# Eight-expert feed-forward stage: second product with tokens on partitions, routing weight as a factor of the row

## The chip, the cores and the metric

The kernel runs on one core of a Trainium2 chip, in float32. The metric is the device time of one launch in microseconds (us). Engines are named as the profile names them: PE (matrix product) and PEld (its weight loads), DVE (vector), ACT (activations), POOL, and SP, which here only issues DMAs.

## The reference

The whole model is a chain of eight residual stages over x of shape (2, 512, 128): attention-like stages and feed-forward stages in turn. The change touches the second one, a feed-forward layer with eight experts of which each token uses two:

```python
xf = x.reshape(-1, D)                       # x is the layernorm of the running sum
scores = xf @ router_w.T
top_v, top_i = jax.lax.top_k(scores, TOP_K) # two of eight
routing_w = jax.nn.softmax(top_v, axis=-1)
out = jnp.zeros_like(xf)
for e in range(NUM_EXPERTS):
    w_e = jnp.sum(jnp.where(top_i == e, routing_w, 0.0), axis=-1)
    h = jax.nn.gelu(xf @ expert_w1[e].T, approximate=False)   # 128 -> 512
    out = out + h @ expert_w2[e].T * w_e[:, None]             # 512 -> 128
# x = x + out
```

Every expert is computed for every token, and the weight w_e is zero where the token did not choose it.

## The kernel before

The running sum X stays in SBUF as 128 partitions x 8 tiles of tokens x 128 features: four token tiles for each of the two batch elements b. The stages run one after the other: stage0 (cross attention with three iterations), stage1 (the eight experts, the one that changes), stage2 (attention with 16 heads), stage3 (experts with one shared matrix and small corrections), stage4 and stage6 (six-layer transformers), stage5 and stage7 (feed-forward stages).

Two things set the order of instructions. Inside `with nc.stretch()` a planner in the kernel records the operations, estimates durations and writes an order of its own; its instructions all carry line 356. Stage 0's iterations, stage 2 and the transformers run so. Outside a stretch, as in all of stage1, the instructions go straight to the framework's scheduler and carry line 124; the scheduler may interleave what does not depend on each other.

Stage1 first takes the layernorm of X, transposes it into nT (features on partitions, 512 tokens per b), computes the scores with the router matrix rw, finds the two best experts on DVE and builds W, the weight of each token for each expert, with tokens on partitions. Then it loops over the experts e and over b; one such pair is called a round below, and there are 16. A round does this:

- four first products of 128x128 weights and 512 tokens go in pairs into two-bank PSUM tiles (`banks()`, name big, two buffers), and one Gelu on ACT for each pair writes hT, hidden features on partitions, tokens along the row;
- a selector product spreads the weight of expert e over all partitions: sel holds one-hot columns of eight rows, wT holds W transposed, and the result is copied from PSUM to wb;
- four second products accumulate over the hidden chunks f into one bank yps (`bank()`, name ms, three buffers), with output features on partitions;
- DVE multiplies yps by wb into y, and POOL adds y to acc.

After the loop acc is transposed back by PE in eight pieces and added to X. An expert's weights, 512 KB, are one DMA on SP's queue into the tile ew, with three buffers; the matrix rw comes by ACT's queue. The tiles of stage1 lie in three pools (one for single tiles, one for double-buffered ones, the expert pool last), which take the SBUF space that the pools of stage0 gave back; a tile waits for what used its place before. Stage2's pools follow in the same way, and its weights wq, wkv and wo are loaded when the places are free.

In the profile one fp32 matmul is shown as two matmul records, each with a weight load of its own.

Of the kernel before, what the change touches and what calls it, by code (L numbers as in the profile page):

```python
# [11 lines left out]
F32 = mybir.dt.float32  # L12
# [3 lines left out]
ALU = mybir.AluOpType  # L16
# [3 lines left out]
P = 128  # L20
D = 128
B = 2
S = 512
NT = S // P
# [9 lines left out]
FC = DFF // P  # L34
# [325 lines left out]
class Kernel:  # L360
# [245 lines left out]
    def stage1(self):  # L606
        nc, X = self.nc, self.X
        E = 8
        with self.tc.tile_pool(name="s1", bufs=1) as one, self.tc.tile_pool(name="s1w", bufs=2) as two, \
                self.tc.tile_pool(name="s1e", bufs=3) as expert:  # L610
            rw = one.tile([P, E], F32, name="rw")
            nc.scalar.dma_start(rw, self.io["router"])
            sel = one.tile([E, E, P], F32, name="sel")
            nc.vector.tensor_copy(sel, self.ident[:E, :E].unsqueeze(2).to_broadcast([E, E, P]))
            nT = [one.tile([P, S], F32, name=f"nT1{b}") for b in range(B)]
            ps = self.bank()
            for b in range(B):
                nc.vector.tensor_copy(nT[b], self.transposed(self.normed(b, X)))
            for t in range(T):
                b, i = divmod(t, NT)  # L620
                nc.tensor.matmul(ps[:, t * E:(t + 1) * E], lhsT=nT[b][:, i * P:(i + 1) * P], rhs=rw, start=True, stop=True)
            sc = one.tile([P, T, E], F32, name="sc1")
            nc.vector.tensor_copy(sc.rearrange("p t e -> p (t e)"), ps[:, :T * E])
            v8, idx = self.top_experts(one, sc, 2)

            dv = one.tile([P, T], F32, name="dv")
            nc.vector.tensor_tensor(dv, v8[:, :, 1], v8[:, :, 0], ALU.subtract)
            nc.scalar.activation(dv, dv, AF.Exp)
            wt = one.tile([P, 2, T], F32, name="wt")
            nc.vector.tensor_scalar(wt[:, 0, :], dv, 1.0, None, ALU.add)  # L630
            nc.vector.reciprocal(wt[:, 0, :], wt[:, 0, :])
            nc.vector.tensor_tensor(wt[:, 1, :], dv, wt[:, 0, :], ALU.mult)
            W = one.tile([P, T, E], F32, name="W1")
            oh = one.tile([P, 2, T, E], F32, name="oh1")
            for k in range(2):
                self.one_hot(oh[:, k], idx[:, :, k])
                nc.vector.tensor_tensor(oh[:, k], oh[:, k], wt[:, k, :].unsqueeze(2).to_broadcast([P, T, E]), ALU.mult)
            nc.vector.tensor_tensor(W, oh[:, 0], oh[:, 1], ALU.add)
            wT = one.tile([E, B, S], F32, name="wT1")
            for b in range(B):  # L640
                ps = self.bank(E)
                for i in range(NT):
                    nc.tensor.transpose(ps[:, i * P:(i + 1) * P], W[:, b * NT + i, :], self.ident)
                nc.vector.tensor_copy(wT[:, b, :], ps)
            acc = one.tile([P, B, S], F32, name="acc1")
            for e in range(E):
                w = expert.tile([P, 1024], F32, name="ew")
                nc.sync.dma_start(w, self.io["w1"][e])
                for b in range(B):
                    hT = two.tile([P, FC, S], F32, name="hT1")  # L650
                    for pair in range(FC // 2):
                        ps = self.banks()
                        for j in range(2):
                            f = 2 * pair + j
                            nc.tensor.matmul(ps[:, j * S:(j + 1) * S], lhsT=w[:, f * P:(f + 1) * P], rhs=nT[b], start=True, stop=True)
                        nc.scalar.activation(hT[:, 2 * pair:2 * pair + 2, :].rearrange("p f s -> p (f s)"), ps, AF.Gelu)
                    wps = self.bank()
                    nc.tensor.matmul(wps, lhsT=sel[:, e, :], rhs=wT[:, b, :], start=True, stop=True)
                    wb = two.tile([P, S], F32, name="wb1")
                    nc.vector.tensor_copy(wb, wps)  # L660
                    yps = self.bank()
                    for f in range(FC):
                        nc.tensor.matmul(yps, lhsT=w[:, 512 + f * P:512 + (f + 1) * P], rhs=hT[:, f, :], start=f == 0, stop=f == FC - 1)
                    if e == 0:
                        nc.vector.tensor_tensor(acc[:, b, :], yps, wb, ALU.mult)
                    else:
                        y = two.tile([P, S], F32, name="y1")
                        nc.vector.tensor_tensor(y, yps, wb, ALU.mult)
                        nc.gpsimd.tensor_tensor(acc[:, b, :], acc[:, b, :], y, ALU.add)
            for b in range(B):  # L670
                pt = self.bank()
                for i in range(NT):
                    nc.tensor.transpose(pt[:, i * P:(i + 1) * P], acc[:, b, i * P:(i + 1) * P], self.ident)
                xb = X[:, b * NT:(b + 1) * NT, :]
                nc.vector.tensor_tensor(xb, xb, pt.rearrange("p (n d) -> p n d", d=D), ALU.add)


    def stage2(self):
# [788 lines left out]
```

## Time and profile before

| | |
|---|---|
| median of 3 runs | 3820.19 us (3816.91 to 3825.85) |
| the profiled execution: its own time, its span | 3818.73 us, 3817.0 us |
| granted PE clock, mean | 0.899 |
| PE busy | 3396.6 us, 89% of the span |
| DVE, ACT, POOL busy | 2449.4, 1762.7, 563.2 us |
| stage1, 163 to 314 us: PE, DVE, ACT, POOL busy | 141.25, 38.37, 35.55, 19.71 of 151 us |

The span is the time from the first to the last instruction; the time of a launch has a little more around it. Busy times are those of one profiled execution. In the lines of a group the columns are the source line, the engine, the operation, output <- inputs, the shapes and the count; after the bar come the busy time in us and the mean duration in ns; after the second bar the idle time of the engine just before these instructions and what ended it. In a timeline the columns are start and duration in us, engine, line, operation and tiles, count, and in brackets the idle time before.

### The profile page before, as it was taken

What the parts mean: (1) busy time and instruction counts of PE and PEld (TensorE: products, weight loads), DVE (VectorE), ACT (ScalarE), POOL (GpSimd) and SP (SyncE); (2) the same over time, 40 slices, a digit from 0 to 9 for tenths busy, and PEclk for the clock granted to TensorE, in tenths of its full rate; (3) what the DMA queues carried; (4) which work ended last, traced back from release to release, by engine and by line L of the source; (5) the groups of instructions that cost most, each with busy time, mean ns of one, the idle gap of its engine ahead of it and who ended that gap; (6) DMA issues with size and microseconds to landing.
All of it is one profiled execution on the core that took longest, in us unless ns stands there. A gap on an engine that the chain in (4) does not pass through costs nothing.

```text
span 3817.0 us, 56843 instructions
## 1 busy us (share of the span) xinstructions
PE 3396.6 (89%) x21539; PEld 1864.8 (49%) x21539; DVE 2449.4 (64%) x5712; ACT 1762.7 (46%) x3268; POOL 563.2 (15%) x516
## 2 busy tenths in 40 slices
PE   5598999889999999999999739999999999999937
PEld 3333555455555455554545425545455455554526
DVE  5514555377676776767677478677676767767532
ACT  1123545236454554545555314456454555545550
POOL 2214767210100000000000010000100001010000
PEclk8698999879898998999989768989899999989858
DMA  1000000100010000000000100010010001000002
GB/s 38 1 28 22 1 1 1 39 12 5 10 25 10 23 7 23 10 10 23 13 7 8 39 5 8 7 28 5 10 25 10 23 7 28 5 10 9 6 20 78
DMA packets 179494, 61.00 MB, mean 16 GB/s; under 512 B 169475, under 2 KB 173367, under 8 KB 177559
## 3 DMA queue, kind: packets, MB, share of 16 engines
q1 hardware_dynamic: 177400, 54.72, 6.4%
q8 instruction: 171, 2.80, 0.3%
q10 hardware_dynamic: 1519, 1.74, 0.1%
q0 software_dynamic: 304, 0.92, 0.1%
q14 instruction: 100, 0.82, 0.1%
HBM read 36.37 MB, written 0.52 MB: 10 GB/s over the span
## 4 chain that ended last, share of the span: by engine, by line
PE 72%; DVE 16%; POOL 4%; ACT 3%; issue 2%; DMA 1%; SPq 1%; DVEq 0%; ACTq 0%; POOLq 0%
PE ms L356 61%; PE ms L124 5%; DVE mx L356 4%; PE big L124 2%; PE av L356 2%; PE big L356 2%; POOL turned L356 2%; POOL p L356 1%; ACT p L356 1%; DVE ln_st L356 1%; DVE nrm L356 1%; POOL ln_rs L356 1%; DVE avT L356 1%; DVE Y L356 1%; SPq L356 1%
## 5 line engine op out<-in xcount | busy, mean ns | idle before, releaser
L356 ACT ACTIVATE p<-ms 128x512 f32<-128x512 f32 (+1 forms) x2304 | 1209.6, 614 | 768.5 <-PE ms L356 764.9
L356 DVE TENSOR_REDUCE mx<-ms 128x1 f32<-128x512 f32 (+2 forms) x2316 | 1281.7, 609 | 238.5 <-PE ms L356 234.4
L356 PE MATMUL ms<-kT,qT 29*128 29x512 f32 x3072 | 949.9, 678 | 30.3 <-DMA qT<-mxT 12.3
L356 PE MATMUL ms<-qT,kT 32*128 32x512 f32 (+1 forms) x3096 | 919.7, 632 | 3.2 <-DVE mx L356 2.7
L356 PEld LDWEIGHTS ms<-kT,qT 29*128 29x128 f32 x3072 | 403.9, 196 | 296.5 <-DVE mx L356 149.9
L356 PEld LDWEIGHTS ms<-qT,kT 32*128 32x128 f32 (+1 forms) x3096 | 376.8, 184 | 190.9 <-issue 61.0
L356 DVE STREAM_TRANSPOSE avT<-ms 128x512 f32<-128x512 f32 x192 | 137.5, 716 | 379.8 <-PE ms L356 379.8
L356 PE MATMUL ms<-kcT,qT 29*128 29x154 f32 x3072 | 353.4, 329 | 25.8 <-DVE mx L356 18.6
L356 POOL TENSOR_TENSOR ln_rs<-ln_ve,mhalf 128x4 f32<-128x4 f32 x96 | 97.5, 1019 | 1851.9 <-DVE ln_ve L356 1851.8
L356 PE MATMUL ms<-p,vp 128*32 128x512 f32 x3072 | 353.2, 600 | 0.7
L356 PE MATMUL ms<-qT,kcT 32*77 32x512 f32 x1536 | 343.6, 641 | 1.5 <-DVE mx L356 1.5
L356 PEld LDWEIGHTS ms<-kcT,qT 29*128 29x128 f32 x3072 | 301.6, 196 | 86.2 <-DVE mx L356 36.0
L356 POOL TENSOR_SCALAR p<-p,s 128x666 f32<-128x666 f32 x128 | 248.8, 1956 | 118.3 <-DVE s L356 118.3
L356 PE MATMUL ms<-p,vcp 77*32 77x512 f32 x1536 | 199.2, 650 | 0.6 <-DVE mx L356 0.5
L356 PEld LDWEIGHTS ms<-p,vp 128*32 128x32 f32 x3072 | 90.9, 110 | 220.7 <-issue 181.7
L356 ACT ACTIVATE nrm_t<-ms,gb 128x512 f32<-128x512 f32 x72 | 56.1, 779 | 290.6 <-PE ms L356 272.9
L356 PE MATMUL ms<-ident,nrm 128*128 128x128 f32 x344 | 83.5, 376 | 96.3 <-DVE nrm L356 79.2
L356 PEld LDWEIGHTS ms<-qT,kcT 32*77 32x77 f32 x1536 | 120.0, 148 | 94.5 <-ACT p L356 32.6
L356 DVE TENSOR_REDUCE m<-big 128x1 f32<-128x666 f32 x128 | 104.2, 847 | 83.0 <-PE big L356 83.0
L356 ACT ACTIVATE p<-big,m 128x666 f32<-128x666 f32 x128 | 103.7, 814 | 116.1 <-DVE m L356 115.3
L356 POOL TENSOR_TENSOR turned<-rope_a,rope_s 128x256 f32<-128x256 f32 x144 | 101.7, 730 | 358.6 <-DVE rope_s L356 358.5
L356 PE MATMUL ms<-nrm_t,lw 128*128 128x512 f32 x192 | 136.0, 874 | 1.7 <-ACT nrm_t L356 1.7
(336 smaller groups left out, 3534.9 us busy)
## 6 DMA issues: line engine op xcount, KB each, us to landing
lw<-in_layers SPq DMA_DIRECT2D x12, 1413.0 KB
ew<-in_w SPq DMA_DIRECT2D x24, 512.0 KB
qT<-rows SPq DMA_DIRECT2D x192, 64.0 KB
qT<-mxT SPq DMA_DIRECT2D x768, 2.0 KB
kT<-rows SPq DMA_DIRECT2D x96, 64.0 KB
wkv<-in_wkv SPq DMA_DIRECT2D x1, 1024.0 KB
f2b<-in_f2b SPq DMA_DIRECT2D x12, 64.0 KB
rv<-in_rows POOLq DMA_DIRECT2D x1, 640.0 KB, 6.5
```

Of the source, the lines that this page charges most:

```text
L124: return getattr(getattr(self._plan.real, self._name), method)(*a, **k)
L356: getattr(getattr(self.real, op.lane), op.method)(*op.a, **op.k)
```

## The change

The second product swaps its operands: a 128-token slice of hT is the stationary operand, and the 128 columns of the second weight matrix are streamed, so that the output has tokens on partitions, the layout of X. Each round then has 16 matmuls of 128 columns instead of four of 512. The routing weight is now one number per partition, so a single DVE instruction for each token tile multiplies the product by a column of W and adds it to X. The tiles sel, wT, wb, y and acc go, with the selector products, the transposes of W and of acc, and POOL's additions.

```diff
--- before.py
+++ after.py
@@ -610,8 +610,6 @@
                 self.tc.tile_pool(name="s1e", bufs=3) as expert:
             rw = one.tile([P, E], F32, name="rw")
             nc.scalar.dma_start(rw, self.io["router"])
-            sel = one.tile([E, E, P], F32, name="sel")
-            nc.vector.tensor_copy(sel, self.ident[:E, :E].unsqueeze(2).to_broadcast([E, E, P]))
             nT = [one.tile([P, S], F32, name=f"nT1{b}") for b in range(B)]
             ps = self.bank()
             for b in range(B):
@@ -636,13 +634,6 @@
                 self.one_hot(oh[:, k], idx[:, :, k])
                 nc.vector.tensor_tensor(oh[:, k], oh[:, k], wt[:, k, :].unsqueeze(2).to_broadcast([P, T, E]), ALU.mult)
             nc.vector.tensor_tensor(W, oh[:, 0], oh[:, 1], ALU.add)
-            wT = one.tile([E, B, S], F32, name="wT1")
-            for b in range(B):
-                ps = self.bank(E)
-                for i in range(NT):
-                    nc.tensor.transpose(ps[:, i * P:(i + 1) * P], W[:, b * NT + i, :], self.ident)
-                nc.vector.tensor_copy(wT[:, b, :], ps)
-            acc = one.tile([P, B, S], F32, name="acc1")
             for e in range(E):
                 w = expert.tile([P, 1024], F32, name="ew")
                 nc.sync.dma_start(w, self.io["w1"][e])
@@ -654,25 +645,15 @@
                             f = 2 * pair + j
                             nc.tensor.matmul(ps[:, j * S:(j + 1) * S], lhsT=w[:, f * P:(f + 1) * P], rhs=nT[b], start=True, stop=True)
                         nc.scalar.activation(hT[:, 2 * pair:2 * pair + 2, :].rearrange("p f s -> p (f s)"), ps, AF.Gelu)
-                    wps = self.bank()
-                    nc.tensor.matmul(wps, lhsT=sel[:, e, :], rhs=wT[:, b, :], start=True, stop=True)
-                    wb = two.tile([P, S], F32, name="wb1")
-                    nc.vector.tensor_copy(wb, wps)
+
                     yps = self.bank()
-                    for f in range(FC):
-                        nc.tensor.matmul(yps, lhsT=w[:, 512 + f * P:512 + (f + 1) * P], rhs=hT[:, f, :], start=f == 0, stop=f == FC - 1)
-                    if e == 0:
-                        nc.vector.tensor_tensor(acc[:, b, :], yps, wb, ALU.mult)
-                    else:
-                        y = two.tile([P, S], F32, name="y1")
-                        nc.vector.tensor_tensor(y, yps, wb, ALU.mult)
-                        nc.gpsimd.tensor_tensor(acc[:, b, :], acc[:, b, :], y, ALU.add)
-            for b in range(B):
-                pt = self.bank()
-                for i in range(NT):
-                    nc.tensor.transpose(pt[:, i * P:(i + 1) * P], acc[:, b, i * P:(i + 1) * P], self.ident)
-                xb = X[:, b * NT:(b + 1) * NT, :]
-                nc.vector.tensor_tensor(xb, xb, pt.rearrange("p (n d) -> p n d", d=D), ALU.add)
+                    for i in range(NT):
+                        for f in range(FC):
+                            nc.tensor.matmul(yps[:, i * D:(i + 1) * D], lhsT=hT[:, f, i * P:(i + 1) * P], rhs=w[:, 512 + f * D:512 + (f + 1) * D],
+                                             start=f == 0, stop=f == FC - 1)
+                    for i in range(NT):
+                        x = X[:, b * NT + i, :]
+                        nc.vector.scalar_tensor_tensor(x, yps[:, i * D:(i + 1) * D], W[:, b * NT + i, e:e + 1], x, ALU.mult, ALU.add)
 
 
     def stage2(self):
```

## The prediction

> **What bounds the kernel now.** I read the page's busy table first (PE 3396.6 us, 89% of the span), then its chain of waits: PE carries 72% of it, and line 124 (everything outside a planned stretch) only "PE ms 5%" and "PE big 2%". The change sits in one such stage, so I left the averages and took the groups and the timeline of 163 to 314 us. The groups:
>
> ```profile
> L124 PE MATMUL big<-nT,ew 128*128 128x512 f32 x128 | 62.2, 627 | 0.8 <-issue 0.8
> L124 PE MATMUL ms<-hT,ew 128*128 128x512 f32 x128 | 59.2, 605 | 0.0
> L124 ACT ACTIVATE hT<-big 128x1024 f32<-128x1024 f32 x32 | 32.8, 1024 | 115.7 <-PE big L124 115.7
> L124 PE MATMUL ms<-wT,sel 8*128 8x512 f32 x32 | 17.9, 640 | 0.0
> L124 POOL TENSOR_TENSOR acc<-acc,y 128x512 f32<-128x512 f32 x14 | 17.7, 1264 | 122.2 <-DVE y L124 89.1 <-issue 33.2
> ```
>
> PE has no idle to speak of; ACT, DVE and POOL all wait for it. Counts are twice the code's (64 second products per stage stand as 128): each fp32 matmul runs as two passes, each with its own weight load. So the stage ends when PE ends. One round (one expert, one batch element), in the timeline (start, duration, engine):
>
> ```profile
> 200.45 1.12 PE L124 MATMUL ms<-wT,sel 8*128 8x512 f32 x2
> 200.56 1.02 ACT L124 ACTIVATE hT<-big 128x1024 f32<-128x1024 f32 x1 [0.63 <-PE big L124]
> 201.50 3.70 PE L124 MATMUL ms<-hT,ew 128*128 128x512 f32 x8
> 202.04 0.19 PEld L124 LDWEIGHTS ms<-hT,ew 128*128 128x128 f32 x1 [0.24 <-issue]
> 202.47 0.19 PEld L124 LDWEIGHTS ms<-hT,ew 128*128 128x128 f32 x1 [0.24 <-issue]
> 205.04 3.60 PE L124 MATMUL big<-nT,ew 128*128 128x512 f32 x8
> 208.57 1.12 PE L124 MATMUL ms<-wT,sel 8*128 8x512 f32 x2
> ```
>
> From selector to selector 8.12 us. A 512-column pass starts every 0.43 us (202.04, 202.47). Sixteen passes are 6.85 us, so the selector's two passes, with the gaps at entering and leaving an 8-row product, take 1.26 us. They also give ACT time: the second Gelu (200.56 to 201.58) runs beside them.
>
> The stage's two ends:
>
> ```profile
> 162.86 0.34 ACTq L124 DMA_DIRECT2D rw<-in_router  x1
> 166.15 0.67 DVE L124 COPY sel<-ident 8x1024 f32<-8x1024 f32 x1
> 171.78 2.04 PE L124 MATMUL big<-nT,ew 128*128 128x512 f32 x2 [0.83 <-issue]
> ...
> 311.56 1.26 POOL L124 TENSOR_TENSOR acc<-acc,y 128x512 f32<-128x512 f32 x1 [6.85 <-DVE y L124]
> 312.88 0.66 PE L124 MATMUL ms<-ident,acc 128*128 128x128 f32 x4 [1.75 <-POOL acc L124]
> 313.70 0.33 SPq L124 DMA_DIRECT2D wkv<-in_wkv  x1
> 320.16 3.57 PE L356 MATMUL ms<-wkv,kv 128*111 128x512 f32 x4 [6.62 <-DMA wkv<-in_wkv]
> ```
>
> The last product ends near 310.54; y, POOL's addition and four transposes follow, and only then is stage 2's weight load wkv issued, for which PE waits. What moves the issue of wkv moves the rest of the kernel.
>
> **What the Trainium skill says.** "TensorE: Matmul & The Clock Gate", section "LDWEIGHTS (loading the stationary operand)": the cost goes by the columns loaded, about columns/1.2 ns, thus an estimated 107 ns for 128. Its "Step-by-step: what each phase is for": the next weights load while the present matmul streams. Both decide here, since the new product has a load for every 128 columns streamed. The trace agrees: two other places of this kernel run that shape (the same loop form at 980 us):
>
> ```profile
> 980.71 3.84 PE L356 MATMUL ms<-lw,hT 128*128 128x128 f32 x32
> 984.48 1.71 PE L356 MATMUL ms<-kcT,qT 29*128 29x154 f32 x32
> 3805.40 7.41 PE L124 MATMUL ms<-eo,put 128*128 128x128 f32 x64 [0.78 <-DVE eo L124]
> ```
>
> 32 passes take 984.48 - 980.71 = 3.77 us (0.118 each); 64 take 7.41 less a last pass of 0.275, over 63: 0.113. A load shows 0.19 us there; it overlaps. "DMA: Bandwidth & Descriptors", "Anatomy of one DMA", gives 2.0 us plus bytes/436e3 for the software path, 3.2 us for a 512 KB expert load as an estimate; here such a load (hardware path) issued at 197.12 had its last data by about 200.1.
>
> **The change part by part.**
>
> *Second product.* 4 matmuls of 512 columns become 16 of 128: 8 passes x 0.43 = 3.42 us become 32 x 0.1155 (mean of the two rows) = 3.70. +0.28 x 16 rounds = **+4.5 us**; ends 0.107 (0.0) and 0.118 (+5.7).
>
> *Selector products.* 16 x 1.26 = **-20.2 us**, all on PE's path.
>
> *Gelu wait.* Without the selector PE comes to the f = 2 weights early. In the built program's order PE issues two second products, then one first product of the next round, then the other fourteen: 4 x 0.1155 + 2 x 0.43 = 1.32 us of cover. The need: Gelu starts 0.21 us after the last first-product pass stops streaming (208.47 to 208.68), takes 1.02, and PE follows an ACT end by 0.05 (in stage 7 an ACT end at 3793.29, PE at 3793.34): 1.28 us, and a weight load that cannot run ahead adds up to 0.1. Behind the waiting load on PE stand the fourteen products and the next first products, and ACT and DVE wait for those. I take 0.1 x 15 = **+1.5 us** (0 to +4). The last round has no next product to put there: 1.38 - 0.46 = **+0.9 us**.
>
> *Start.* The sel copy goes (0.67 us on DVE ahead of the layernorm that gates PE): **-0.65**. The eight transposes of W go from PE: **-0.9** (0.8 to 1.0, with the wT copies beside). Four passes come while PE is still at half clock (0.853 against 0.43 us a pass until 183.7): **+0.2**.
>
> *End.* From 310.54 to the wkv issue is 3.16 us now. After: 0.2 drain, four row updates, 0.13 to the issue. SCALAR_TENSOR_TENSOR of 128x128 from PSUM is in stage 0: 0.348 us, three in 0.88, so four in 1.15. 1.5 us in all: **-1.65**. The four wait together for the last matmul in the built order. Ahead of them in DVE's queue stands batch 0's first layernorm of stage 2 (some 5.2 us with POOL's 1.02), which starts about 7 us before PE ends, when batch 0's own updates are done; if it is late it costs up to 1 us.
>
> *First expert load.* Fewer tiles lie below the expert pool, so in the built program the first ew lands where stage 0's tiles lay, and its load, issued at 4.25 us now, waits for stage 0's last slots instruction. rw waits for the same one now: 162.86 us. Behind it on SP stand only the other two ew loads. Three loads together moved 414 to 422 GB/s between 9 and 12 us of the span; the first should land by 166.5, all three by 168. PE asks at 171.1. **0**, with 4.6 us to spare.
>
> *DVE and POOL.* Per round 1.15 us of row updates for 1.38 (wb and y), POOL's 1.26 gone, against a round of 7.2: hidden behind PE; the three ms banks come free sooner. The X rows are chained on DVE alone. **0**.
>
> Sum: 4.5 - 20.2 + 1.5 + 0.9 - 0.65 - 0.9 + 0.2 - 1.65 = **-16.3 us**. Rounds fall from 8.12 to 7.22. Stage 2 and what follows keep their order and move as a block. The profiled execution took 3818.73 us around its span of 3817.0; it becomes 3802.4. The median of the runs shown is 1.5 us above it (3820.19): **3803.9**.
>
> **The rivals.**
>
> *Gelu exposed.* If the load after the wait and the semaphore cost 0.5 us more a round, as where PE enters the selector and its loads show 0.76 us of issue idle instead of 0.24, 8 us go: 3812. Against it: that gap comes with the change to 8 rows, and the filler is there in the order.
>
> *Weight loads exposed: slower.* Were load and stream in series, 0.19 + 0.107 = 0.30 us a pass, a product would take 9.5 us and 512 passes 94 us more than I count: 3898. It decides from a pitch of 0.148 us (16.3 us over 512 passes). For it: every pass has a new weight tile, read from the hT that ACT is writing. Against: both rows above, each with a new tile per pass.
>
> *The load of ew late.* If three loads share the engines so that the first ends with the third, and slowly, PE starts up to 4 us later: 3808. Against: even the third should be there 3 us early.
>
> *Gained in the stage, lost behind.* PE idles some 8 us for wkv instead of 6.6 and starts stage 2 in another phase of its clock (granted 0.79 there); the end could move by 3 us either way. The runs before span 9 us themselves. That the change removes less than it says is excluded by the built order: no sel, wT, acc or wb instruction is left.
>
> **How the numbers follow.** Main case 0.80: 3803.9, with its unknowns (pitch 0 to +5.7 in place of 4.5, Gelu 0 to +4, DVE to +1, clock 3 either way) 3796 to 3810. Gelu exposed 0.10, ew late 0.05, weight loads exposed 0.02, else 0.03. Range 3796 to 3811. A measurement of this kernel tells 0.2% (7.6 us) from no change, so faster means below 3812.6: main and ew, most of Gelu exposed: 0.93; same 0.05; slower 0.02.
>
> **What would show it.** Right: 512 passes ms<-ew,hT 128x128 at 0.113 to 0.118 us; rounds of 7.1 to 7.4; PE idle before a load with releaser ACT hT below 0.2 us a round; ew issued near 162.8 and no PE wait for DMA ew; wkv issued near 297.4. Wrong: a pitch above 0.13, an ACT hT wait of 0.5, a PE wait for ew, or stages 2 to 7 longer than now by more than 3 us.

## The result, and the profile after

The changed kernel takes **3794.64 us** (median of 22 runs, 3780.85 to 3825.77), the kernel before in the same comparison 3816.26 (22 runs): ratio 0.995, 95% interval 0.9932 to 0.9969, or 12 to 26 us. Two later comparisons of the same pair, a1_new and a2_new, gave 0.9949 [0.9930, 0.9967] and 0.9939 [0.9916, 0.9962]. The forecast was 3803.9, or -16.3, with a range of 3796 to 3811.

The two profiled executions differ by 37.9 us (3817.0 and 3779.1 of span), and that must not be read as the gain of the stage. Here are four stretches cut at the same events of both traces, with a third execution beside them (a1_new, the changed kernel again). "Slots" below is the start of stage 0's last slots<-s1c instruction, its output's layernorm:

| us | before | after | a1_new |
|---|---|---|---|
| start of the span to slots | 162.3 | 161.9 | 166.2 |
| from there to the first scores product of stage 2 (big<-kT,qT) | 171.96 | 153.75 | 155.41 |
| from there to the transformer's first weight load | 384.30 | 385.73 | 384.13 |
| from there to the output | 3091.43 | 3070.73 | 3081.35 |

The change shows in the second stretch: -18.2 and -16.6. The 1.6 us between these two lie mostly behind the stage, from the issue of wkv to the scores product (20.99 and 22.28 us), where PE's granted clock stood at half for 10.2 us in the one execution and 13.7 us in the other. The last stretch holds no changed instruction and differs by over 10 us between two executions of one kernel. I therefore measure the stage from the release that both kernels have at its start (rw before, ew after, both waiting for stage 0's slots) to the issue of wkv: 313.70 - 162.86 = 150.84 before, 294.66 - 162.36 = 132.30 after, **-18.5 us**.

The groups of the changed kernel between 163 and 300 us (columns as in the section on the profile before):

```profile
L124 PE MATMUL big<-nT,ew 128*128 128x512 f32 x128 | 64.4, 626 | 0.9 <-issue 0.9
L124 PE MATMUL ms<-ew,hT 128*128 128x128 f32 x512 | 63.9, 278 | 0.7 <-ACT hT L124 0.7
L124 PEld LDWEIGHTS ms<-ew,hT 128*128 128x128 f32 x512 | 61.4, 193 | 18.5 <-ACT hT L124 13.8 <-issue 4.2 <-ACT dv L124 0.5
...
L124 DVE SCALAR_TENSOR_TENSOR X<-ms,W,X 128x128 f32<-128x128 f32 x64 | 18.0, 344 | 89.3 <-PE ms L124 89.3
```

The reader is to see three things. The selector's group is gone. The new product has 512 passes and 63.9 us busy, hardly more than the 59.2 of the 128 long ones, though a single pass shows 278 ns: passes overlap, so the mean of one is not the pitch, the step from the start of one pass to the start of the next. And PEld waits 13.8 us for Gelu (ACT hT) where PE waits 0.7: most of the time in which a weight load waits is covered by what PE still streams. Not all of it, as the next view shows.

One round in the timeline of the changed kernel, with one row of PEld:

```profile
203.72 0.61 PE L124 MATMUL ms<-ew,hT 128*128 128x128 f32 x4
203.91 1.02 ACT L124 ACTIVATE hT<-big 128x1024 f32<-128x1024 f32 x1 [0.63 <-PE big L124]
204.16 1.02 PE L124 MATMUL big<-nT,ew 128*128 128x512 f32 x2
204.99 3.20 PEld L124 LDWEIGHTS ms<-ew,hT 128*128 128x128 f32 x28 [0.64 <-ACT hT L124]
205.02 3.37 PE L124 MATMUL ms<-ew,hT 128*128 128x128 f32 x28
...
208.22 2.74 PE L124 MATMUL big<-nT,ew 128*128 128x512 f32 x6
...
210.80 0.61 PE L124 MATMUL ms<-ew,hT 128*128 128x128 f32 x4
```

From 203.72 to 210.80 is 7.08 us (8.12 before). 28 passes take 208.22 - 205.02 = 3.20 us, 0.114 each on average; in the steady part of the run one starts every 0.112 us. The Gelu of 203.91 ends at 204.93; the 28 passes that need it begin at 205.02, with nothing in brackets: the two 512-column passes of the next round, put between, keep PE busy through the wait. They are called the filler below.

The filler does not quite cover the weight load. In the steady part a load starts as the pass before it does; this one starts at 204.99, after Gelu, only 0.03 us before its pass. So the first of the 28 passes lasts 0.349 us where the others last 0.275, and the second starts 0.185 us after it in place of 0.112. That is 0.07 us in each of 14 rounds which no column of idle time shows (round 1 has its Gelu early, and the last round waits openly). The four row updates follow the last pass, at 208.42, beside the next round.

The ends of the stage, changed kernel:

```profile
162.36 1.30 SPq L124 DMA_DIRECT2D ew<-in_w  x3
...
170.84 2.04 PE L124 MATMUL big<-nT,ew 128*128 128x512 f32 x2 [0.90 <-issue]
...
289.99 3.39 PE L124 MATMUL ms<-ew,hT 128*128 128x128 f32 x28 [0.67 <-ACT hT L124]
...
293.42 1.12 DVE L124 SCALAR_TENSOR_TENSOR X<-ms,W,X 128x128 f32<-128x128 f32 x4 [1.13 <-PE ms L124]
294.66 0.33 SPq L124 DMA_DIRECT2D wkv<-in_wkv  x1
...
301.12 3.72 PE L356 MATMUL ms<-wkv,kv 128*111 128x512 f32 x4 [7.75 <-DMA wkv<-in_wkv]
```

The three expert loads now go out at 162.36 instead of 4.25 us, and PE still does not wait for them: "issue" is the releaser at 170.84, as before. The last round alone has no filler, and PE stands idle for 0.67 us before its 28 passes. The last product ends near 293.2, wkv is issued 1.46 us later, and its data is used 6.46 us after the issue, as in the kernel before (320.16 - 313.70).

### The profile page after: what moved, and what is told of

Same layout as the page of the kernel before. It is cut to its first block, busy times and chain, and to the rows that moved or that the text cites. A ratio compares the mean times of both kernels' runs of the same rounds, so it can differ in the third digit from the quotient of the medians.

```text
span 3779.1 us, 57532 instructions
## 1 busy us (share of the span) xinstructions
PE 3361.6 (89%) x21875; PEld 1885.6 (50%) x21875; DVE 2440.3 (65%) x5739; ACT 1760.8 (47%) x3268; POOL 545.6 (14%) x502
## 4 chain that ended last, share of the span: by engine, by line
PE 67%; DVE 14%; POOL 4%; ACT 3%; issue 2%; DMA 1%; SPq 1%; DVEq 0%; POOLq 0%; ACTq 0%
PE ms L356 59%; DVE mx L356 3%; PE ms L124 2%; PE av L356 2%; PE big L356 2%; POOL turned L356 2%; POOL p L356 1%; ACT p L356 1%; DVE ln_st L356 1%; DVE nrm L356 1%; DVE avT L356 1%; DVE Y L356 1%; PE big L124 1%; SPq L356 1%; POOL ln_rs L356 1%
```

## The experiments

Of e1 to e5 there is one execution each (3810.61, 3793.73, 3801.59, 3816.05 and 3816.43 us in the order of their numbers). As totals these tell nothing, since 22 runs of one kernel spread over 45 us; the five are read by the stage in their traces.

**a1_new and a2_new: the changed kernel again**, as the reference of its comparison (results above). Edit: none. Expected:

> The new kernel again, beside the two below on one chip. Theory: its stage 1 is 18.5 us shorter (slots to wkv 132.3 against 150.8 us in every execution, within 0.3), and stages 2 to 7 take the same, so the ratio to the old kernel is 0.995 and what single executions show beyond it (38 us in the two profiled ones) is the spread of the granted clock behind stage 1. Rival: stages 2 to 7 gain as well, another 5 to 15 us, in this profile too.

> The new kernel once more, beside the next on one chip. Ratio to the old kernel 0.995 within its interval; slots' last start to wkv 132.8 to 133.1 us; slots' last start to the first q-k product of stage 2 about 154 us; the time from the first transformer weight load to the output between 3070 and 3102 us, since the same code has shown these ends in the runs so far.

What follows: the gain repeats. The stage took 132.64 us in a1_new and 132.33 in a2_new (from the issue of ew to that of wkv), against 132.30; a1_new lies 0.04 us outside the 0.3 that were expected. From slots to the first scores product a2_new took 153.8 us, and from the transformer's first weight load to the output 3084.2, both as expected.

Whether stages 2 to 7 gain as well, the rival in a1_new's text, cannot be read from single executions: that last stretch is 10.1 us shorter than before in a1_new and 7.3 in a2_new, but it spreads over 31 us in all the executions below. Runs of the two kernels can also be compared at one granted clock. The regressions of time on mean clock pass, at a clock of 0.898, through 3817.8 for the kernel before (23 runs) and 3799.1 for the changed one (13 runs) in a1_new's comparison, and through 3818.7 (15 runs) and 3799.0 (10 runs) in a2_new's: -18.7 and -19.7 us, close to the stage's own figure. When 18.5 us at full clock go, the mean clock itself falls by an estimated 0.0005, worth 1.6 us at 33 us for each 0.01, so this bears out the size to about 2 us and no closer.

**e1_selector_back: what does the selector cost in the new kernel?** The other parts stay changed. The product's result is copied and not used.

```diff
+            sel = one.tile([E, E, P], F32, name="sel")
+            nc.vector.tensor_copy(sel, self.ident[:E, :E].unsqueeze(2).to_broadcast([E, E, P]))
...
+                    wps = self.bank()
+                    nc.tensor.matmul(wps, lhsT=sel[:, e, :], rhs=nT[b][:E, :], start=True, stop=True)
+                    wb = two.tile([P, S], F32, name="wb1")
+                    nc.vector.tensor_copy(wb, wps)
```

> The new kernel with a selector product of 8 rows and its copy to wb put back into every round; nothing reads wb, so the result is the same. Only the price of the selector in PE's stream is asked for. Theory (the selector cost 1.26 us a round, two passes of 0.43 and the gaps of entering and leaving an 8-row product): rounds of 7.09 + 1.26 = 8.35 us, and the time from stage 0's last slots instruction to the issue of wkv grows from 132.3 to about 152.5 us. Rival (the gaps belonged to the Gelu wait and to the old order, the selector itself is two passes): rounds of 7.95, 146 us. Rival (PE was not the bound, the removed DVE and POOL work gave the gain): rounds stay at 7.1.

A round in its timeline, PE's matmuls alone:

```profile
207.49 1.12 PE L124 MATMUL ms<-nT,sel 8*128 8x512 f32 x2
208.54 3.84 PE L124 MATMUL ms<-ew,hT 128*128 128x128 f32 x32
212.21 3.60 PE L124 MATMUL big<-nT,ew 128*128 128x512 f32 x8
215.74 1.12 PE L124 MATMUL ms<-nT,sel 8*128 8x512 f32 x2
```

8.25 us, 1.17 more than 7.08, and the stage 18.2 us longer than in the changed kernel (151.0 from slots to wkv, against 132.76); 0.5 us of that is the sel copy ahead of the first product. The selector costs PE nearly its full price here. Its passes do cover Gelu, and the scheduler puts no filler in; the 0.07 us that the filler had left uncovered are gone, which is most of what is missing to 1.26. The rival in which DVE and POOL had set the pace (rounds of 7.1) is refuted.

**e2_old_no_selector: the old orientation without the selector in each round.** The weights of expert 0 are spread once, before the loop, for all rounds, so that the weighting by expert is left out.

```diff
+            wbs = []
+            for b in range(B):
+                wps = self.bank()
+                nc.tensor.matmul(wps, lhsT=sel[:, 0, :], rhs=wT[:, b, :], start=True, stop=True)
+                wb = one.tile([P, S], F32, name=f"wb1{b}")
+                nc.vector.tensor_copy(wb, wps)
+                wbs.append(wb)
...
-                    wps = self.bank()
-                    nc.tensor.matmul(wps, lhsT=sel[:, e, :], rhs=wT[:, b, :], start=True, stop=True)
-                    wb = two.tile([P, S], F32, name="wb1")
-                    nc.vector.tensor_copy(wb, wps)
+                    wb = wbs[b]
```

> The old kernel (output features on partitions, acc by POOL, transposes at the end) with the selector product taken once before the loop and not in every round. It leaves out the change of weight by expert: every round is scaled by expert 0's weights. Theory: the selector is all that the loop gains; without it the old product needs 16 x 0.43 = 6.85 us a round, less than the new kernel's 7.09, since its two f = 0, 1 products last 1.7 us and cover the Gelu (1.28). Stage time, slots to wkv: 150.8 - 15 x 1.26 = 131 to 132 us, of which the end (y, POOL, transposes, 3.2 us) is still there. Rival (the Gelu wait was hidden by the selector alone): rounds of 7.3 or more.

Its timeline, PE's matmuls alone:

```profile
205.29 3.60 PE L124 MATMUL ms<-hT,ew 128*128 128x512 f32 x8
208.72 3.60 PE L124 MATMUL big<-nT,ew 128*128 128x512 f32 x8
212.15 3.60 PE L124 MATMUL ms<-hT,ew 128*128 128x512 f32 x8
```

6.86 us a round: the selector was worth 8.12 - 6.86 = 1.26 us in the old kernel, the prediction's price. The swap of operands by itself makes a round longer, 7.08 - 6.86 = 0.22 us or 3.5 us in 16.

The stage from slots to wkv is 134.07 us and not the 131 to 132 that were expected: two selector products still stand before the loop, so 14 of 16 are gone and not 15, and 151.4 - 14 x 1.26 = 133.8. That is 1.3 us more than in the changed kernel; without the two it would be an estimated 131.5, 1.2 us less. So the swap loses 3.5 us in the rounds and 0.9 at the last Gelu, and gets most of that, not all, back at the stage's ends, where the sel copy, the transposes and POOL's addition were. The gain is the selector's going; what the orientation buys is that the weight needs no spreading. A cheaper way to spread it in the old orientation was not tried.

**e4_as_written: no filler.** The loop keeps its written order.

```diff
+            with self.tc.manual_schedule():
...
```

> The new kernel with the loop over the experts in the order in which it is written: no first product of the next round stands between the second and the third second product. Theory (that first product hides the Gelu): the wait that the last round of the new kernel shows, 0.67 us of PE, comes in every round: 7.09 + 0.67 = 7.76 us, the stage 15 x 0.67 = 10 us longer, 142 us; PE idle with releaser ACT hT about 11 us in place of 0.7. Rival (the wait is short anyway, a weight load is pulled ahead): rounds below 7.3. Rival (a wait costs a pipeline refill as well): 8.0 or more.

Its timeline, PE's second products alone:

```profile
205.79 0.61 PE L124 MATMUL ms<-ew,hT 128*128 128x128 f32 x4
...
207.07 3.39 PE L124 MATMUL ms<-ew,hT 128*128 128x128 f32 x28 [0.67 <-ACT hT L124]
...
213.73 0.61 PE L124 MATMUL ms<-ew,hT 128*128 128x128 f32 x4
```

Its view of waits from 163 to 320 us (engine and tile <- releaser: us in all, times, longest):

```profile
PE ms L124 <- ACT hT L124: 10.4, 16, 0.7
```

A round is 7.94 us, between the theory's 7.76 and the second rival's 8.0, and the stage 145.37 us from slots to wkv, 12.6 longer. All 16 rounds now wait, where the changed kernel waited once.

The idle shown is 0.67 us a round, the loss 0.86. The rest can be read from the single passes. Idle is counted from the end of the pass before, but a pass lasts 0.275 us and the next would have started 0.112 after it: from there to 207.07 PE is 0.83 us late. The load that follows starts late too, so that the next pass comes 0.213 us after in place of 0.112, another 0.10. Against this go the 0.07 us that the round with the filler loses: 0.83 + 0.10 - 0.07 = 0.86. In the written order the change would have gained 18.5 - 12.6, some 6 us; twice that hangs on the order that the scheduler writes.

**e5_half_columns: is the pass set by its stream or by its weight load?** Only 64 of the 128 output features are computed; the other half is left out.

```diff
-  nc.tensor.matmul(yps[:, i * D:(i + 1) * D], ..., rhs=w[:, 512 + f * D:512 + (f + 1) * D],
+  nc.tensor.matmul(yps[:, i * D:i * D + 64], ..., rhs=w[:, 512 + f * D:512 + f * D + 64],
```

> The new kernel with only 64 of the 128 feature columns of the second product streamed and added to X; it leaves out the other 64. Theory (a pass is bound by its weight load, 128 columns in about 0.107 us, as the 64-column passes of stage 7 at 0.115 us hint): the pitch stays at 0.113 to 0.115 and the rounds at 7.0 to 7.1. Rival (bound by the stream): a pitch near 0.055 to 0.06, rounds of 5.3 us plus what the shorter cover leaves of the Gelu.

Its timeline, PE's matmuls and one row of PEld:

```profile
199.92 3.23 PE L124 MATMUL ms<-ew,hT 128*128 128x64 f32 x28
199.92 3.09 PEld L124 LDWEIGHTS ms<-ew,hT 128*128 128x128 f32 x27 [0.24 <-issue]
...
202.99 1.94 PE L124 MATMUL big<-nT,ew 128*128 128x512 f32 x4
```

28 passes of half the columns take 202.99 - 199.92 = 3.07 us, where 28 whole ones took 3.20. The steady step is 0.112 us in both runs. The difference lies at the first pass: the scheduler puts four filler passes here and not two, so that the first load comes in good time, and the second pass starts only 0.056 us after the first, which is what 64 columns take at the rate of the 512-column pass (0.43 / 8 = 0.054). So no fixed cost holds a pass to 0.11 us. Behind it the loads, which start 0.11 us apart, set the pace.

The stream of 64 columns is thus not what sets the pass; the 128-column weight load is. This is the figure of the Trainium skill, "TensorE: Matmul & The Clock Gate", section "LDWEIGHTS (loading the stationary operand)": columns/1.2 ns, an estimated 107 ns. The trace agrees to 5 ns, and in its columns: a load's record lasts 0.110 us for 32 columns and 0.190 for 128 (medians of ms<-p,vp and big<-nT,ew in the kernel before), 0.83 ns a column. At 128 streamed columns the two are about equally long, since a quarter of the 0.43 us for 512 columns is 0.107 us: that is why the swap costs so little.

**e3_early_load: the first expert loads early again.** A tile of 20 KB that nothing else uses is put below the expert pool, so that ew lies where it lay before.

```diff
+            pad = one.tile([P, 5120], F32, name="pad")
+            nc.gpsimd.memset(pad[:, 5119:5120], 0.0)
```

> The new kernel with an unused tile of 20 KB a partition below the expert pool, so that the expert tiles lie above stage 0's again and their loads are issued at the start, near 4 us. Theory (the first load lands 4 us before PE asks): nothing changes, PE's first product at 170.8 us less the shift of stage 0, slots to wkv 132.3 us within 0.3. Rival (the late load delayed the first product): the stage is 1 to 4 us shorter.

The first load goes out at 4.20 us; from rw's issue at 166.12 to wkv's at 298.41 is 132.29 us, against 132.30 from the issue of ew in the changed kernel. The late load costs nothing, as the prediction had it.

**e6_weights_early: the wait for wkv that stands behind the stage.** Stage 2's wq, wkv and wo go into a pool that is opened ahead of stage 1, and their loads are written into the third expert's turn of the loop. SP runs ahead of PE: wkv is issued at 168.23 us, before the stage's first product.

```diff
+        with self.tc.tile_pool(name="s2k", bufs=1) as keep:
+            wq = keep.tile([P, 1024], F32, name="wq2")
...
+            self.stage1()
+            self.stage2()
...
+                if e == 2:
+                    self.load2()
```

> The new kernel with stage 2's weights wq, wkv and wo in a pool opened before stage 1's, loaded during the third expert in place of after the last update of X. Theory: PE waits 7.75 us for wkv in the new kernel; without it the first wkv product starts right after stage 1's last product, and the second layernorm, which stands behind the copy of that product on DVE, follows at once: 7.5 to 9 us off, ratio to the old kernel about 0.993, the wait of PE for DMA wkv gone. Next late would be that layernorm. Rival (the layernorm of batch 0 is as late as the weights): 1 us or less. Rival (the loads collide with the expert loads): a PE wait for DMA ew in expert 3 or 4.

Its timeline at the end of the stage:

```profile
294.46 1.13 DVE L124 SCALAR_TENSOR_TENSOR X<-ms,W,X 128x128 f32<-128x128 f32 x4 [5.96 <-PE ms L124]
295.51 0.35 DVE L356 TENSOR_SCALAR kv<-ctx_nrm_t,cv 128x154 f32<-128x154 f32 x1
...
295.96 1.94 PE L356 MATMUL ms<-wkv,kv 128*111 128x512 f32 x4 [1.53 <-issue]
...
296.03 0.29 DVE L356 BATCH_NORM_STATS2 ln_st<-X 128x6 f32<-128x128 f32 x1
```

PE no longer waits for wkv, yet little of the expected 7.5 to 9 us came. From slots to the scores product it is 148.98 us instead of 153.75, but most of these 4.8 us arose at the start of the stage: PE's granted clock stood at half for 2.9 us after the stage's first product in this execution and for 12.3 us in the changed kernel's, and the stage's last product ends 128.0 us after slots and not 131.5. Behind the last product only 1.3 us are won (20.96 us to the scores product, against 22.27), nearly the first rival's "1 us or less".

The layernorm of batch 0, which had run beside the last round (287.38 in the changed kernel), now starts at 296.03, behind the last updates. Ahead of it in DVE's planned order stands the write of kv, and the tile kv now lies where stage 1's expert tiles were, so it waits for PE's last product (in the changed kernel it was written at 169.80). PE then waits 4.7 us for the layernorm's result, nrm. In e3_early_load kv and the layernorm were as late (298.16 and 298.68) at no cost, as PE was waiting for wkv anyway. Moving one set of tiles moved the place of another, and made a new wait. In the total nothing can be told: 3801.38 (11 runs), ratio 0.996 [0.9937, 0.9982] to the kernel before, against a1_new's 0.9949.

**e7_weights_and_kv_early: as e6, with the two kv tiles in the early pool as well.**

```diff
+            self.kv2 = [keep.tile([P, SC + S], F32, name=f"kv2{b}") for b in range(B)]
...
-                    kv = two.tile([P, NK], F32, name="kv2")
+                    kv = self.kv2[b]
```

> The kernel with stage 2's weights early once more, with the kv tiles also in the pool opened before stage 1's. In the run before, the weights did come early, but kv then lay on the expert tiles, and its write, which stands before batch 0's first layernorm on DVE, waited for stage 1's last product: that layernorm started after the last update of X in place of 7 us before it. Theory: with kv out of the way the layernorm runs beside the last round again (as in the new kernel), PE starts wkv within 2 us of the last product, and from slots' last start to the first q-k product it is 144 to 147 us against 154; ratio to the old kernel near 0.9925. Rival (PE is as late by the second layernorm's pow on POOL and the v copies): 149 us, as in the run before.

Its timeline at the same place:

```profile
287.89 0.86 DVE L356 BATCH_NORM_STATS2 ln_st<-X 128x6 f32<-128x128 f32 x4
...
289.67 1.02 PE L356 MATMUL ms<-wkv,kv 128*111 128x512 f32 x2
...
307.54 1.39 PE L356 MATMUL big<-kT,qT 64*128 64x512 f32 x8
```

The layernorm is back beside the last round, a product of stage 2 fills part of that round's wait for Gelu (289.67), and the scores product comes 307.54 - 162.3 = 145.24 us after slots: -8.5 against the changed kernel. All of it lies behind the last product, 13.65 us to the scores product in place of 22.27, and the half clock at the stage's start lasted 12.3 us as in the changed kernel. In that stretch the granted clock is 1.00, where it was 0.77 with the wait for wkv; how much of the 8.6 us is the wait and how much the clock is not told apart. The cause found in e6 is thereby shown. The total, 3794.53 (6 runs), has a ratio to the kernel before of 0.9916 [0.9883, 0.9949], beside 0.9939 [0.9916, 0.9962] of a2_new in the same comparison. The two overlap widely: the 8.5 us show in the stage's trace, but that the whole kernel is faster than the changed one by them is not shown.

## Why the prediction was right, step by step

The mechanism and the bound were right: PE sets the stage's end, and what leaves PE's path comes out of the time. Its terms against the traces:

| step | predicted | measured | from |
|---|---|---|---|
| selector gone | -20.2 | -20.2 (16 x 1.26) | e2 |
| second product | +4.5 at 0.1155 a pass | +2.3 (16 x 0.14, at 0.112 a pass) | steady step |
| Gelu wait in the rounds | +1.5 (15 x 0.1) | +1.0 (14 x 0.07) | the step of 0.185 |
| last round | +0.9 | +0.9 (0.67 idle, 0.83 + 0.10 in all) | 289.99, e4 |
| transposes of W, half clock | -0.9, +0.2 | -0.4 together (the remainder) | |
| first to last product in all | -14.0 | -16.4 (171.78 to 310.54; 170.84 to 293.2) | ends |
| start of the stage | -0.65 | -0.44 (rw or ew to the first product: 8.92 and 8.48) | 170.84 |
| end of the stage | -1.65 | -1.70 (3.16 to 1.46) | 294.66 |
| ew late, DVE, POOL | 0 | 0 | e3, e1, groups |
| sum | -16.3 | -18.5 | |

The two measured terms of the round, 0.14 and 0.07 us, make up the 0.22 us that e2 gives for the swap. In e1 the selector's price is 1.17 us a round, since there it takes the 0.07 away.

**The sum was 2.2 us short, and the term that was mis-sized is the second product.** The pitch was taken as the mean over two rows of other stages, 0.1155, and the difference to the old product came out twice too large. In these rows, too, the steady step was 0.112: each held single longer steps (one of 0.214 us) which the mean spread over all passes. The Gelu term was right in its kind. The prediction set the cover (1.32) just above the need (1.28), so that PE would not stand idle, and added up to 0.1 for a weight load that cannot run ahead; that is what the trace shows, 0.07. The half microsecond by which this term was too dear and the half by which the start and the transposes brought less than forecast cancel.

**The rest of the 9 us between forecast and median** is not a step of the sum, and that the range holds it is not clear-cut. The median lies 1.4 us below 3796. The median before, 3820.19, came from three runs; 22 runs gave 3816.26, and counted from there the range is 3792 to 3807. From there -16.3 would be 3800, and the stage's own -18.5 gives 3797.8, 3 us above the median, inside what the interval leaves open. The forecast's word that stages 2 to 7 move as a block holds in the order of instructions, but for the first write of kv (at 169.80 us and no longer at 312.87). As a time it cannot be read from single executions: the span's last stretch fell by 20.7 us in the profiled one and by 10.1 in a1_new.

**The rivals.** *Gelu exposed* (3812): its price, 0.5 us a round, was rather low, since a round without the filler is 0.86 us longer (e4), but its case did not occur: what stood against it, the filler in the order, decided. *Weight loads exposed* (3898): refuted by the pitch, 0.112 against a break-even of 0.148 (0.1155 + 16.3 / 512 is 0.147). *ew late* (3808): refuted by the "issue" at 170.84 and by e3. *Lost behind*: small. From the issue of wkv to the scores product it took 20.56 us before, 20.99 and 22.28 after (a1_new), within the 3 us that the prediction allowed for another phase of the clock; the stretch behind it took 384.30 before, 385.73 and 384.13 after.

## What to carry to other kernels

Price a matmul with a fresh 128-column weight tile per pass at its load or its stream, whichever is longer. At 128 streamed columns of fp32 the two are about equal here, so turning a product around for a cheaper layout costs little, and pays if it takes another product off the bound engine; at 64 columns nothing more was saved (e5). Take the pitch from the steady part of a row, not from its mean. Before an edit removes work from PE, look for what that work covered and whether the built order has something else to put there; here 0.86 us a round hung on it. And a tile that moves takes others with it: after any change of pools, look again at which earlier tile each load and write now waits for. When two traces are compared by a stretch, look at the granted clock in both first; in e6 it was worth more than the edit.

## What the runs showed of the hardware that was not expected

With a new 128-column weight load for each, passes of 64 and of 128 streamed columns both start every 0.112 us; with the load in time, the pass after one of 64 columns came 0.056 us later (e5). An 8-row product of two 512-column passes costs 1.25 us on PE where two such passes among equals cost 0.86: the four steps into, in and out of it are 0.52 to 0.53 us in place of 0.43. A wait for Gelu that shows as 0.67 us of idle puts the passes behind it 0.93 us back (e4). And a weight load that comes late can cost PE 0.07 us with no idle shown at all.

The largest is the spread of unchanged work. From the transformer's first weight load to the output, stages 4 to 7, the same code in all eleven executions traced here, took 3070.7 to 3101.6 us. The clock granted to PE is 1.0 or 0.5 in these traces and nothing between; in that stretch it stood at 0.5 for 614 to 676 us, and the stretch's length follows this time with a correlation of 0.97, 0.49 us for each us. Over 22 runs of the changed kernel the time follows the mean granted clock of the run (0.890 to 0.903) with a correlation of -0.95, 33 us for each 0.01. In each trace the changes of the clock lie whole multiples of 3.413 us apart (in the changed kernel at 159.2, 183.1, 295.7 and 305.9 us: 7, 33 and 3 of them), and where these multiples fall differs between executions: in stage 1 the half clock lasted from 2.9 us (e6) to 12.9 us (a1_new) after the first product. The Trainium skill, "TensorE: Matmul & The Clock Gate", section "What's actually happening", has the clock gated by PE's recent activity; what makes the time at half clock differ between runs of one program no run here shows. An edit worth 20 us in such a kernel is best measured by stretches of the trace and by many runs, and not by two executions.
